# A causal attention block with sixteen routed experts on one core: turns, products and copies in other places of the issue order

## Chip, cores and metric

One of the cores of a Trainium2 chip runs the whole program in one launch. The metric is the device time of that core in microseconds (us). The kernel before takes 1741.03 us, the median of three runs (1738.7 to 1745.79). All arithmetic is in 32-bit floats.

## What is computed

```python
# x: 4 sequences of 1024 tokens, 256 wide; 16 heads of 64
proj = x @ W_in.T + b_in                      # q, k, v of all heads
q, k = rope(q, sin, cos), rope(k, sin, cos)   # y_lo = lo*cos + hi*sin; y_hi = hi*cos - lo*sin
att = softmax(mask(q @ k.T / 8))              # causal
x = layernorm(x + (att @ v) @ W_out.T + b_out)
gates = top 3 of softmax(x @ gate), scaled to sum to 1      # of 16 experts
x = layernorm(x + sum over the 3 of gate * (relu(x @ W1 + b1) @ W2 + b2))
```

## The kernel before, in words

**Two halves.** `attention` (from line 89) works through 32 pairs of heads, n = 0 to 31, eight pairs to a sequence. `moe` (from line 830) then works through 56 tiles of 256 tokens, each with one expert's weights. In both, the order of the instructions on TensorE (PE) is the order in which they are written. The other engines' order comes from a scheduler that takes what is ready first, within the ties that the program adds. Each engine then runs its own list in order, and waits on semaphores where an operand or a buffer isn't free.

**A pair has six slots**, k = 0 to 5 (loop at line 432). The 1024 queries of the pair are cut into eight chunks of 128; `chunks` (line 411) gives slot 0 chunk 7, slot 1 chunk 6, slot 2 chunk 5, slot 3 chunk 4, slot 4 chunks 3 and 2, and slot 5 chunks 1 and 0. In a slot:

- `scores` (line 279) multiplies q and k on PE into PSUM tiles of 512 columns (tag "s"). For each tile VectorE (DVE) scales, masks and takes the row minimum of the negated scores (line 308, tile `nmax`), writing P to SBUF. ScalarE (ACT) takes the exponential (line 323). `divide` (line 334) has DVE invert the row sums (line 337) and GpSimd (POOL) multiply P by them (line 340).
- `turn` (line 349) has DVE transpose P in blocks of 32, two slots after its scores, into `t_first` (keys 0 to 511) or `t_last` (keys 512 to 1023). `rows` holds the turns of a slot, and `turns` takes off the first entry, for both heads.
- `product(n, j)` (line 364) is P times V on PE for key chunk j. Slots 3, 4, 5 take j = 7, 6, 5 of pair n; slots 0, 1, 2 of the next pair take 4 and 3, 2, 1 and 0. It reads V from `vr`.
- `out` (line 397) is the output projection of two row blocks, summed into `acc` by DVE (line 468, called the sum here).
- `project(n+1, i, g)` (line 198) makes half g of the next pair's q (i = 0) or k (i = 1): four matmuls into a PSUM tile `pp` (also tag "s"); DVE's bias-and-sin product (line 220); ACT's plain copy with bias, `rawq` or `rawk` (line 226); and, once the tile is whole, four DMAs that write it back with its 32-row blocks swapped, `swq` or `swk` (line 234). k is projected in slots 0 and 1, so `swk` is issued in slot 1; q in slots 2 and 5. `rotate` (line 236) multiplies the swapped copy by cos and adds it, on DVE for k of pair 0 and on POOL otherwise.
- `values` (line 247) projects V, and DMAs write it to DRAM (`v_d`). `spread(n, g)` (line 271) loads half g back with four DMAs of 256 KB, one to each block of 32 partitions: `vr`. The four for g = 1, issued in slot 1, serve products 7 to 4; the four for g = 0, issued in slot 4, serve 3 to 0. There is one buffer for each g.

**PSUM.** All tiles of tag "s" share four buffers, in turn: scores, `pp`, `oo` of the output projection and `vv` of the values. In slot 0 they are four score tiles, `oo`, `pp`; slot 1's four score tiles so take the buffers of slot 0's third and fourth score tile, its `oo` and its `pp`.

**The SyncE (SP) queue** issues nearly all DMAs, in order; one that has to wait holds those behind it. `late(...)` (line 118) ties a DMA behind whatever was written last for the same queue, so the scheduler can't pull it forward. Loads of `wo` (line 143), `vr` (line 275), the third use of `wqk` and later (line 135) and `wv` are tied so; the `swk` and `swq` copies are not tied themselves.

**Orders by hand.** `after(i, kind)` (line 330) puts an instruction behind the last one of that kind in the issue order, with no wait. `divide` comes last in a slot, and `project` of k is tied behind the inverse.

**One-time steps.** `residual` (line 175) adds the output bias to half of `acc` on POOL. `plan` holds the router's steps; `first[2]` turns the first list of token numbers on PE (line 798). `moe.run` (line 949) gathers and loads six tiles, calls `last_norm` (the layernorm of the last sequence, lines 70 to 86) through `begun`, and then turns the first tile of tokens on PE and DVE (lines 884 and 886).

Of the kernel before, what the change touches and what calls it, by code (L numbers as in the profile page):

```python
# [88 lines left out]
def attention(  # L89
# [4 lines left out]
    nc = tc.nc  # L94
    with ExitStack() as ctx:
# [17 lines left out]
        ps_s = pool("ps_s", 4, space=PSUM)  # L113
# [84 lines left out]
        def project(n, i, g, kind=None):  # L198


            b, p = divmod(n, NP)
            if i == 0:
                half = rot[n, 0, g] = qkp.tile([P, 512], FP, tag=f"rotq{g}", name="rotq")
                part = raw = qkp.tile([P, 512], FP, tag="rawq", name="rawq")
                whole = True
            else:
                whole = (n, 1) in rot
                if not whole:
                    rot[n, 1] = qkp.tile([P, T], FP, tag="rotk", name="rotk")
                    raws[n] = qkp.tile([P, T], FP, tag="rawk", name="rawk", bufs=1)  # L210
                half, raw = rot[n, 1][:, ts(g, 512)], raws[n]
                part = raw[:, ts(g, 512)]
            ps = ps_s.tile([P, 512], FP, tag="s", name="pp")
            for c in range(DC):
                nc.tensor.matmul(  # L215
                    ps, lhsT=wqk[n][:, c, i, :], rhs=xts[b, g][:, c, :],
                    start=(c == 0), stop=(c == DC - 1),
                )
            bias = bqk[:, i, p : p + 1]
            m = nc.vector.scalar_tensor_tensor(  # L220
                half, ps, bias, sin[:, ts(g, 512)], ALU.add, ALU.mult
            )
            if kind:
                after(m, kind)
                order["part"] = m
            nc.scalar.activation(part, ps, AF.Identity, bias=bias)
            if whole:

                if i == 0:
                    swp = swps[n, 0, g] = qkp.tile([P, 512], FP, tag="swq", name="swq")  # L230
                else:
                    swp = swps[n, 1] = qkp.tile([P, T], FP, tag="swk", name="swk", bufs=1)
                for r in range(4):
                    nc.sync.dma_start(out=swp[ts(r, 32), :], in_=raw[ts(r ^ 1, 32), :])

        def rotate(n, i, g=None):
            key = (n, i) if i else (n, i, g)
            swp, res = swps.pop(key), rot[key]
            eng = nc.vector if n == 0 and i else nc.gpsimd
            first = eng.tensor_tensor(  # L240
                swp, swp, cos if i else cos[:, ts(g, 512)], ALU.mult
            )
            if "divide" in order:
                after(first, "divide")
            eng.tensor_tensor(res, res, swp, ALU.add)  # L245
# [175 lines left out]
        plan = {}  # L421
# [5 lines left out]
        with tc.manual_schedule(engines={mybir.EngineType.PE}):  # L427
            for n in range(n_pairs + 2):
                b, p = divmod(n, NP)
                if n == 2:  # L430
                    load_router()
                for k in range(n_slots):
                    here, before, ahead = (one_of(n + i) for i in (0, -1, 1))
                    part, ends, last = None, [], "scores"
                    if k == 2 and before:
                        product(n - 1, 1)
                    if here:
                        ends = scores(n, chunks[k])

                    m, kk = divmod(n * n_slots + k - 2, n_slots)  # L440
                    rows = [(qc, h) for h in (1, 0) for qc in chunks[kk] if qc >= 4 * h]

                    def turns(last):
                        qc, h = rows.pop(0)
                        for hh in range(2 if one_of(m) else 0):
                            turn(m, qc, hh, h, last)
                            last = "turn"
                        return last

                    if k == 2:  # L450
                        last = turns(last)

                    if k in (2, 5) and ahead:
                        project(n + 1, 0, int(k == 2), last)
                        last = "part"
                    if k < 3 and before:
                        product(n - 1, (4, 2, 0)[k])
                        if k == 2:
                            close(n - 1)
                    if k >= 3 and here:  # L460
                        product(n, 10 - k)
                    if k in (0, 3, 4, 5) and one_of(n - 1 - (k == 0)):
                        part = out(n - 1 - (k == 0), (k - 3) % 4 if k else 3)
                    if k != 2:
                        last = turns(last)
                    if part:
                        a, ps = part
                        order["sum"] = after(nc.vector.tensor_tensor(a, ps, a, ALU.add), last)
                        last = "sum"
                    while rows:  # L470
                        last = turns(last)
                    divide(n, ends, last)

                    if k == 0 and one_of(n + 2) and n % 2 == 0:
                        late(load_v(n + 2))
                    if k == 1 and one_of(n):
                        late(load_o(n))
                        spread(n, 1)
                        if one_of(n + 2):
                            late(load_qk(n + 2))  # L480
                    if k == 4 and one_of(n):
                        spread(n, 0)

                    if ahead:
                        if k < 2:
                            project(n + 1, 1, k, "inverse")
                        elif k == 2:
                            rotate(n + 1, 1)
                        elif k == 3:
                            rotate(n + 1, 0, 1)  # L490
                    if k == 0 and one_of(n):
                        rotate(n, 0, 0)
                    if k == 0 and before:
                        product(n - 1, 3)
                    m = n + 2 - n % 2
                    if k in (3, 4) and one_of(m):
                        values(m, 2 * (n % 2) + k - 3)
                    if k in (1, 2) and n == 0:
                        values(0, k - 1)
                    if k in (0, 4):  # L500
                        if n < 2 and k == 4 * (1 - n):
                            residual(0, n)
                        if p == NP - 1 and b + 1 < B:
                            residual(b + 1, k // 4)
                    for go in plan.pop((n, k), []):
                        go()
                    if k == 1 and p == 1 and 0 < b < B:
                        normalise(b - 1, sp)
                        steps, place, scatters = router.batch(
                            b - 1, accs[b - 1], ps_s, "s", ps_s, "s"  # L510
                        )
                        for i, go in enumerate(steps):
                            plan[n + i // 2, (3, 5, 1, 3)[i]] = [go]
                        plan[n + 2, 3] = [place]
                        for i in range(3):
                            for slot, c0, c1 in ((0, 0, 2), (1, 2, 4), (5, 4, 8)):
                                plan[n + 3 + i, slot] = scatters[8 * i + c0 : 8 * i + c1]
                        if b == B - 1:
                            plan[n + 6, 1] = [lambda: first.extend(router.first_list())]
                            plan[n + 6, 3] = [  # L520
                                lambda: first[1](router.on_dve), lambda: first[2](ps_s, "s")
                            ]
                if b + 1 < B:
                    if p == 3:
                        load_acc(b + 1)
                    if p == 4:
                        late(load_x(b + 1, 0))
                    if p == 6:
                        late(load_x(b + 1, 1))
            assert not plan  # L530
# [299 lines left out]
def moe(tc, router, first, last_norm, acc, ident, eps_t, wall, x_a, x_b, sums, out):  # L830
    nc = tc.nc
    with ExitStack() as ctx:
# [116 lines left out]
        def run(t0, t1, begun=lambda: None):  # L949
            with tc.manual_schedule(engines={mybir.EngineType.PE}):  # L950
                for t in range(t0, t0 + 6):
                    gather(t)
                    if t < t0 + 4:
                        load(t)
                begun()
                turn(t0)
                for t in range(t0, t1):
                    if t + 4 < t1:
                        load(t + 4)
# [171 lines left out]
```

## Time and profile before

| what | value |
|---|---|
| median of three runs | 1741.03 us (1738.7 to 1745.79) |
| time of the profiled execution | 1742.73 us |
| its span, first to last instruction | 1740.8 us |
| mean granted clock of TensorE | 0.969 |
| busy in the span: DVE, ACT, POOL | 1169.2, 716.2, 1106.4 us |
| HBM read and written | 183.17 and 52.79 MB |

The profile is one execution, times counted from the start of its span. A line of the timeline gives start, duration, engine, source line, operation, output tile <- input tiles, shape and count, and in brackets the idle time of the engine just before it with what ended it. PEld is the load of weights into TensorE, which runs beside the matmuls; SPq is SP's issue of DMAs, which is not the transfer itself. Matmuls are pipelined, and one that waits inside a group makes the group longer, without a bracket.

### The profile page before, as it was taken

Reading aid. Unit: us, or ns where it says so; the run is one execution under the profiler, and the core shown is the slowest. Engines: PE = TensorE matmul, PEld = TensorE weight load, DVE = VectorE, ACT = ScalarE, POOL = GpSimd, SP = SyncE. Lnnn points to the kernel's source line nnn. Section 1 sums busy time; section 2 is a strip of 40 time slices with the busy share of each in tenths; the row PEclk is TensorE's granted clock in tenths of the full one; section 3 lists DMA queues with packets and bytes.
Section 4 is the critical chain, followed back from the end, with each engine's and each line's share of the span. In section 5 each row is a group of like instructions: output and inputs, shape, how many; then the busy total and the mean of one; then the engine's idle time right before and its main releaser. Section 6 shows DMA issues by size and latency. Waiting matters only on the chain. (4 is left out here: it accounts for less than half of the span.)

```text
span 1740.8 us, 51881 instructions
## 1 busy us (share of the span) xinstructions
PE 1606.5 (92%) x20920; PEld 1097.8 (63%) x20920; DVE 1169.2 (67%) x3516; ACT 716.2 (41%) x1634; POOL 1106.4 (64%) x1050
## 2 busy tenths in 40 slices
PE   7899999989899998989999898999899999999970
PEld 3556556656556565655655565565588888888860
DVE  4678878888888788888887888888655222222224
ACT  3445445544444455445454554454322222222214
POOL 2656565754468865646786454588557778888544
PEclk9999999999999999999999999999899999999995
DMA  6454644464355546535554553444668998989857
GB/s 186 110 144 123 166 120 123 120 198 110 93 134 142 127 111 187 126 83 141 128 144 117 145 154 96 102 119 103 206 202 191 227 241 245 246 238 245 215 96 268
DMA packets 118166, 272.96 MB, mean 157 GB/s; under 512 B 21873, under 2 KB 72433, under 8 KB 102562
## 3 DMA queue, kind: packets, MB, share of 16 engines
q1 hardware_dynamic: 93122, 239.91, 49.8%
q0 software_dynamic: 24656, 29.68, 9.4%
q8 instruction: 167, 2.74, 0.7%
q14 instruction: 77, 0.63, 0.1%
q10 hardware_dynamic: 144, 0.01, 0.0%
HBM read 183.17 MB, written 52.79 MB: 136 GB/s over the span
## 5 line engine op out<-in xcount | busy, mean ns | idle before, releaser
L340 POOL TENSOR_SCALAR p<-p,rinv 128x512 f32<-128x512 f32 (+7 forms) x512 | 374.8, 747 | 436.0 <-DVE rinv L337 432.0
L323 ACT ACTIVATE p<-p,nmax 128x512 f32<-128x512 f32 (+7 forms) x512 | 391.9, 766 | 468.3 <-DVE nmax L308 446.9
L300 PE MATMUL s<-rotk,rotq 64*128 64x512 f32 (+3 forms) x1536 | 338.1, 522 | 21.9 <-POOL rotq L245 10.3
L357 DVE STREAM_TRANSPOSE t_first<-p 128x512 f32<-128x512 f32 (+3 forms) x512 | 276.7, 583 | 26.9 <-PE y_ps L378 26.3
L215 PE MATMUL pp<-xT,wqk 128*128 128x512 f32 x512 | 258.6, 630 | 35.8 <-DVE nmax L308 20.5
L300 PEld LDWEIGHTS s<-rotk,rotq 64*128 64x128 f32 x1536 | 152.7, 188 | 172.2 <-issue 96.9
L378 PEld LDWEIGHTS y_ps<-t_first,vr 32*64 32x64 f32 x8192 | 164.6, 133 | 101.3 <-DVE t_first L357 31.3
L378 PE MATMUL y_ps<-t_first,vr 32*64 32x160 f32 (+1 forms) x8192 | 222.0, 346 | 4.0 <-DVE t_first L357 3.8
L308 DVE CUSTOM_DVE_ANT_0 p<-s,zero 128x512 f32<-128x512 f32 x256 | 165.6, 683 | 87.6 <-PE s L300 87.6
L901 ACT ACTIVATE hid<-ps,w 128x256 f32<-128x256 f32 x224 | 93.9, 470 | 314.6 <-issue 252.2
L917 DVE TENSOR_TENSOR y<-ps,w 128x512 f32<-128x512 f32 x56 | 38.7, 691 | 274.5 <-PE ps L912 274.5
L926 POOL DMA_INDIRECT sums<-y,ids x112 | 178.4, 1592 | 69.1 <-DVE y L922 37.8
L896 PE MATMUL ps<-xg,w 128*128 128x256 f32 x896 | 204.4, 382 | 2.7 <-DVE xg L886 2.7
L912 PE MATMUL ps<-w,hid 128*128 128x256 f32 x896 | 202.6, 379 | 0.0
L912 PEld LDWEIGHTS ps<-w,hid 128*128 128x128 f32 x896 | 169.9, 190 | 22.9
L896 PEld LDWEIGHTS ps<-xg,w 128*128 128x128 f32 x896 | 167.1, 191 | 23.7 <-DVE xg L886 2.9
L215 PEld LDWEIGHTS pp<-xT,wqk 128*128 128x128 f32 x512 | 92.2, 195 | 130.7 <-issue 67.2
L378 PEld LDWEIGHTS y_ps<-t_last,vr 32*64 32x64 f32 x7424 | 113.7, 133 | 79.4 <-issue 64.4
L400 PE MATMUL oo<-wo,yT 128*128 128x256 f32 x512 | 147.1, 412 | 6.4 <-DVE nmax L308 4.6
L378 PE MATMUL y_ps<-t_last,vr 32*64 32x96 f32 (+3 forms) x7424 | 139.5, 253 | 3.3 <-ACT yT L391 0.6
L308 DVE CUSTOM_DVE_ANT_0 p<-s,mask,nmax 128x512 f32<-128x512 f32 (+3 forms) x256 | 130.3, 546 | 0.9 <-issue 0.5
L254 PE MATMUL vv<-wv,xT 128*128 128x256 f32 x512 | 121.3, 380 | 4.8 <-DVE nmax L308 4.8
(147 smaller groups left out, 1890.3 us busy)
## 6 DMA issues: line engine op xcount, KB each, us to landing
vr<-v_d SPq DMA_DIRECT2D x256, 256.0 KB
w<-in_wall_dram SPq DMA_DIRECT2D x56, 1154.0 KB
swk<-rawk SPq DMA_DIRECT2D x128, 128.0 KB
swq<-rawq SPq DMA_DIRECT2D x256, 64.0 KB
v_d<-v SPq DMA_DIRECT2D x128, 128.0 KB
wqk<-in_w_qk_dram SPq DMA_DIRECT2D x32, 256.0 KB
xT<-in_xT_dram SPq DMA_DIRECT2D x8, 512.0 KB
wv<-in_w_v_dram SPq DMA_DIRECT2D x16, 256.0 KB
```

Of the source, the lines that this page charges most:

```text
L215: nc.tensor.matmul(ps, lhsT=wqk[n][:, c, i, :], rhs=xts[b, g][:, c, :], start=(c == 0), stop=(c == DC - 1),)
L254: nc.tensor.matmul(ps[:, u, :], lhsT=xts[b, cc // 2][:, c, ts(cc % 2 * 2 + u, P)], rhs=wv[n][:, c, :], start=(c == 0), stop=(c == DC - 1),)
L300: nc.tensor.matmul(s[:, :n_k], lhsT=rot[n, 0, qc // 4][ts(hh, KD), ts(qc % 4, P)], rhs=k[ts(hh, KD), ds(k0, n_k)], start=True, stop=True,)
L308: i = nc.vector.tensor_tensor_reduce(out=probs[n, qc, hh][:, ds(k0, n_k)], in0=s[:, :n_k], in1=mask[:, 512 - n_k :] if last else zero[:, : ...
L323: nc.scalar.activation(pr, pr, AF.Exp, bias=m, scale=-1.0, accum_out=rsum[:, hh : hh + 1])
L340: order["divide"] = router.behind = nc.gpsimd.tensor_scalar(pr, pr, rinv[:, hh : hh + 1], 1.0, ALU.mult, ALU.mult)
L357: order["turn"] = router.on_dve = after(nc.vector.transpose(turned[n][h][:, hh, :, ds(i - 4 * h, n_j, step=7 - 4 * h), :], probs[n, i, hh] ...
L378: nc.tensor.matmul(st[n][a][ts(hh, KD), ds(32 * j, 32 * (TC - j))], lhsT=vrs[n, h][ts(a, 32), jh // 2 * 8 + 2 * u + jh % 2, ts(hh, KD)], r ...
L400: nc.tensor.matmul(ps[:, v, :], lhsT=st[n][:, ts(2 * h + v, P)], rhs=wo[n], start=True, stop=True,)
L896: nc.tensor.matmul(ps[:, f - f0, :], lhsT=w[:, ds(c * FF + f * P, P)], rhs=xg[:, c, :], start=(c == 0), stop=(c == DC - 1),)
L912: nc.tensor.matmul(ps[:, h, :], lhsT=hid[:, f, ts(h, P)], rhs=w[:, ds(W2_AT + f * D, D)], start=(f == 0), stop=(f == FC - 1),)
L926: s = behind(nc.gpsimd.indirect_dma_start(out=sums[t % 2], out_offset=bass.IndirectOffsetOnAxis(ap=ids[:, h, i : i + 1], axis=0), in_=y[:, ...
```

## The change

- In slot 5 the first turn goes ahead of the bias-and-sin product of q, as it already did in slot 2; the second turn then comes ahead of the sum.
- In slots 0 and 1 the projection of the next pair's k is written directly behind the sum (slot 0) or the first turn (slot 1), ahead of the remaining turns and of the inverse. It was written behind `divide` and behind the loads of `wo`, `vr` and `wqk`. All that `project` issues moves with it: the four matmuls, DVE's product, ACT's copy, and in slot 1 the four `swk` DMAs. PE's order stays as it was, as nothing else for PE lay between.
- The swap copies of q of pair 0 are issued from ACT's queue instead of SP's; k of pair 1 is rotated on DVE instead of POOL.
- The two bias sums of the first sequence move from pair 0 slot 4 and pair 1 slot 0 to pair 1 slot 5 and pair 2 slot 4.
- The turn of the first token list moves from slot 3 to slot 4 of pair 31.
- In `moe.run` the turn of the first tile goes ahead of `begun`, the last layernorm.

```diff
@@ project
+                eng = nc.scalar if n == 0 and i == 0 else nc.sync
                 for r in range(4):
-                    nc.sync.dma_start(out=swp[ts(r, 32), :], in_=raw[ts(r ^ 1, 32), :])
+                    eng.dma_start(out=swp[ts(r, 32), :], in_=raw[ts(r ^ 1, 32), :])
@@ rotate
-            eng = nc.vector if n == 0 and i else nc.gpsimd
+            eng = nc.vector if n < 2 and i else nc.gpsimd
@@ the loop over slots
-                    if k == 2:
+                    if k in (2, 5):
                         last = turns(last)
...
-                    if k != 2:
+                    if k != 2 and rows:
                         last = turns(last)
                     if part:
                         a, ps = part
                         order["sum"] = after(nc.vector.tensor_tensor(a, ps, a, ALU.add), last)
                         last = "sum"
+
+                    if k < 2 and ahead:
+                        project(n + 1, 1, k, last)
+                        last = "part"
                     while rows:
                         last = turns(last)
                     divide(n, ends, last)
...
                     if ahead:
-                        if k < 2:
-                            project(n + 1, 1, k, "inverse")
-                        elif k == 2:
+                        if k == 2:
                             rotate(n + 1, 1)
...
+                    if (n, k) in ((1, 5), (2, 4)):
+                        residual(0, n - 1)
                     if k in (0, 4):
-                        if n < 2 and k == 4 * (1 - n):
-                            residual(0, n)
...
-                            plan[n + 6, 3] = [
-                                lambda: first[1](router.on_dve), lambda: first[2](ps_s, "s")
-                            ]
+                            plan[n + 6, 3] = [lambda: first[1](router.on_dve)]
+                            plan[n + 6, 4] = [lambda: first[2](ps_s, "s")]
@@ moe.run
+                turn(t0)
                 begun()
-                turn(t0)
```

## The prediction

> **What bounds the kernel now.** I read the page first, then PE's timeline through the attention half, then the other engines and SP's queue over one pair, and the windows for what the DMA engines carry.
>
> ```profile
> PE 1606.5 (92%) x20920; PEld 1097.8 (63%) x20920; DVE 1169.2 (67%) x3516; ACT 716.2 (41%) x1634; POOL 1106.4 (64%) x1050
> ```
>
> PE is the longest by far, so an edit pays only where PE stands, or runs slow inside a group. The chain that ended last covers 2% of the span and only the last layernorm, so it doesn't help here. An undisturbed pair in PE's timeline, slots 1 to 4:
>
> ```profile
> 251.74 2.59 PE L300 MATMUL s<-rotk,rotq 64*128 64x512 f32 x8
> 254.26 1.56 PE L378 MATMUL y_ps<-t_first,vr 32*64 32x192 f32 x64
> 255.75 1.98 PE L215 MATMUL pp<-xT,wqk 128*128 128x512 f32 x4
> 257.66 1.77 PE L378 MATMUL y_ps<-t_first,vr 32*64 32x224 f32 x64
> 259.36 1.56 PE L300 MATMUL s<-rotk,rotq 64*128 64x512 f32 x8
> 261.27 1.99 PE L215 MATMUL pp<-xT,wqk 128*128 128x512 f32 x4 [0.35 <-DVE nmax L308]
> 263.19 1.98 PE L378 MATMUL y_ps<-t_first,vr 32*64 32x256 f32 x64
> 265.10 1.35 PE L300 MATMUL s<-rotk,rotq 64*128 64x512 f32 x8
> 266.38 1.15 PE L378 MATMUL y_ps<-t_last,vr 32*64 32x32 f32 x40
> ...
> 270.24 1.77 PE L300 MATMUL s<-rotk,rotq 64*128 64x512 f32 x8
> ```
>
> Groups follow one another with one bracket of 0.35 in 35.85 us. But the first score group (slot 1) takes 2.59 where the last (slot 4, also 512 and 384 columns for both heads) takes 1.77: 0.8 us are lost inside. PE's weight loads name the cause:
>
> ```profile
> 253.42 0.29 PEld L300 LDWEIGHTS s<-rotk,rotq 64*128 64x128 f32 x2 [0.53 <-ACT rawk L226]
> ```
>
> The fourth score tile takes the PSUM buffer of slot 0's `pp`, which ACT's copy frees only at 253.37. That copy follows DVE's product at 251.91, which stands behind the sum (250.35), two turns (1.02) and the inverse. So DVE's order in slot 0 costs PE 0.8 us. PE's timeline lists 19 such whole slot 1 groups (2.46 to 2.60); with those split by a query's edge I count 21 of 32 pairs.
>
> Now SP's queue:
>
> ```profile
> 96.15 2.47 SPq L234 DMA_DIRECT2D swq<-rawq  x4
> 98.67 0.58 SPq L549 DMA_DIRECT2D dump<-in_dump_dram  x1
> ...
> 248.76 0.36 SPq L143 DMA_DIRECT2D wo<-in_w_outT_dram  x1
> 249.16 1.86 SPq L275 DMA_DIRECT2D vr<-v_d  x4
> 251.07 0.42 SPq L135 DMA_DIRECT2D wqk<-in_w_qk_dram  x1
> 259.30 2.41 SPq L234 DMA_DIRECT2D swk<-rawk  x4
> ```
>
> The `vr` of products 7 to 4 is asked for at 249.16, as soon as product 4 of the pair before has freed the buffer, and product 7 (40 matmuls at 266.38) needs all four parts: 17.2 us of room. SP then stands until ACT's second `rawk` (258.55, 0.69 long). The first two lines show that a tied load keeps its place: `dump` waits for nothing, and yet goes out right behind the swaps written before it. The windows show what the transfer takes:
>
> ```profile
> 250.00:256.00 6.00, 6.00 (x139) 3.56 (x138) 5.75 (x17) 2.86 (x6) 3.83 (x4) 1.00 1.02 233
> 256.00:257.00 1.00, 1.00 (x3) 0.42 (x3) 0.35 (x2) 1.00 (x2) 0.90 (x1) 1.00 0.09 29
> 257.00:260.00 3.00, 3.00 (x70) 1.73 (x70) 0.92 (x2) 0.71 (x2) 2.00 (x2) 1.00 0.00 0
> ```
>
> The last two columns are the DMA engines' share and GB/s: full for 6.0 us, 233 GB/s x 6 = 1.40 MB, which is `wo` + 4 `vr` + `wqk` (0.125 + 1.05 + 0.26), then nothing. By proportion `vr` has landed by 250 + 6 x 1.18/1.44 = 254.9, at the latest at 256.1: 5.8 to 6.9 us behind its first issue. I take 6.4.
>
> **The change, part by part.**
>
> *k's product behind the sum, slot 0.* DVE can start it when the sum (about 250.95) and `pp` (about 250.4) are done, so 1.0 sooner; ACT's copy ends near 252.4 and not 253.37. The fourth tile's first load would want it about 252.9. The two turns and the inverse move 0.7 later; DVE stood 0.25 before slot 1's first reduction and ACT's exponential had ended, so nothing becomes late, and POOL, which stood 3.77 before that division, has room. Gain 0.8 a pair, and about 0.05 from product 3, which just waited for a turn: 0.85 x 21 = **-18**. If DVE had no room, the 0.7 would return as later reductions and the gain would be near zero.
>
> *The turn sooner, slot 5.* DVE stood 0.72 for `pp` and 0.87 for `oo` there; turns of 0.49 and 1.29 fill both. The sum still starts about when `oo` is done (280.4 against 280.49), and DVE is free for slot 0 about 1 us sooner. This is cover for the step above and is already in it: 0. Without that cover (pairs with router work on DVE) the sum is 1.3 late, and so is a buffer of slot 0: up to +1.3 in six pairs, down to 0; I take 0.
>
> *k's project in slot 1: its four DMAs.* Here more moves than DVE's product. `swk` is now written ahead of `wo`, `vr` and `wqk`, and these are tied behind what SP was given last. SP so waits for `rawk` first, and the three loads stand behind it, whose buffers have been free for 10 us. Counted in this pair's times: `rawk` ends 259.24, `swk` is issued 259.30 to 261.71, `wo` takes 0.36, the first `vr` goes out about 262.1 and the fourth lands 6.4 later at 268.5. PE wants it at 266.38: **a wait of 2.1 us** that isn't there today. DVE can't shorten it: its product already follows `pp` at once in slot 1 (0.55 of idle for PE), and both ends move together if slot 1's scores get faster. In the other pairs the end of the `swk` issues lies 2.0 to 5.4 ahead of product 7 (middle 4.66, mean 4.2), so the wait is 0.4 + 6.4 less that: mean 2.6. Some issues are slow where other transfers were in flight, so I take 2.3; bounds 1.4 (landing in 5.8, usual distance) and 3.3 (landings of 7 to 8 us). Pairs 0 to 30 have it: 31 x 2.3 = **+71**. Nothing later gives it back: output, values and slot 4's scores follow on PE, and DVE and POOL only get slack.
>
> [...]
>
> *Pair 0 to 1.* PE stands longest here:
>
> ```profile
> 60.02 3.79 PE L300 MATMUL s<-rotk,rotq 64*128 64x512 f32 x8 [6.28 <-POOL rotq L245]
> ```
>
> POOL had k's rotation (2.37 + 2.35) and a bias sum (2.34) ahead of that rotation of q; both leave, 7.1 in all, so the 6.3 go. DVE gets 1.22 + 1.23 (its rows for pair 0's rotation) in slots 2 to 3, where it stood only 0.33; up to +2.1 if PE followed at once, down to 0 because product 7 waits for `vr` then: I take 0. The bias sum in pair 2 slot 4 can hold that pair's next sum: divisions end near 280 in the pattern above, plus 2.35 is 282.3 against a sum at 280.4: +1.5. Together **-5**. The q swaps on ACT start at about 14.9 and not 15.78, but hold ACT's next copies 0.6 each: -0.9 to +1, taken as 0.
>
> *One-time turns.* `ids` (PE idle 2.35 at 1236.47): its data is there by slot 4, **-2**. The last norm: PE stood 2.65 before 1269.67 for a DVE copy behind 2.70 + 0.62 of statistics: **-2**, between -2.6 and 0. Pair 2's slot 1, where `rawk` was late by 1.45: **-1**.
>
> Sum: 71 - 18 - 5 - 2 - 2 - 1 = +43. The profiled execution is 1742.7 (span 1740.8 and 1.9 around), so 1786; the median of the runs is 1.7 below it, so **1784**.
>
> **Rivals.**
>
> *The loads are in time (faster).* Either the scheduler issues `vr` at its old place, or the four parts land within 4.3 us (266.4 - 262.1). Then only the gains are left: 1741 - 28 = 1713. [...] Against it: the tied loads keep their place wherever I looked[...]. The point of decision is 4.3 us from first issue to landing.
>
> *Wait and gain cancel.* A landing in about 5.1 us gives 0.8 to 0.9 of wait a pair (31 x 0.9 = 28) against 28 of gains: 1741. Nothing in the row is that fast.
>
> *The wait is larger and gains are lost.* If landings take 7.4 (other transfers in the same stretch) the wait is 3.3: 102 - 28 = +74, 1815. Against: the DMA engines were idle from 257 to 260 and only `swk` is ahead.
>
> **Chances.** Forecast case 0.80 (about 1760 to 1806: waits of 1.6 to 3.0), in time 0.10, cancelled 0.05, larger 0.05. The range 1750 to 1810 leaves out the first rival and the top. Faster by over 0.5% (8.7 us, about what a measurement of this kernel can tell from no change) 0.10, within 0.05, slower 0.85.
>
> **What would show it.** Right: in SP's timeline `swk`, then `wo`, `vr`, `wqk`; PE idle about 2 us before `y_ps` with `t_last` 32x32 in every pair, put down to the DMA of `vr`; slot 1's scores at 1.7 to 1.8; no 6.28 at pair 1; ACT's `rawk` behind DVE's product as before. A pair of 37.2 to 37.5 us for 35.85. Wrong: `vr` still issued in slot 0, or that product starting with no idle time; or slot 1's scores still at 2.6, which would mean that another buffer held them.

## The result, and the profile after

The changed kernel takes **1904.18 us** (median of four runs, 1897.27 to 1913.42) where the kernel before, run beside it, takes 1742.99 (1738.7 to 1745.79): a ratio of 1.0944, interval 1.0917 to 1.0971, so 161 us slower. 43 were forecast. The profiled execution took 1909.57 us; its span is 1907.8 us, the mean granted clock of TensorE (the share of its full speed at which it was let run) 0.922, for 0.969 before. Executions over 1.5% longer than the shortest of the same kernel are left out of the times and ratios below (on the chip of 1821.92 us eleven of the kernel before, with a granted clock of 0.946 to 0.951, where the others had 0.951 to 0.959).

From the page of the kernel before, the groups to compare (busy time and mean ns of one, then the idle time just before them with what ended most of it):

```profile
L378 PE MATMUL y_ps<-t_last,vr 32*64 32x96 f32 (+3 forms) x7424 | 139.5, 253 | 3.3 <-ACT yT L391 0.6
L400 PE MATMUL oo<-wo,yT 128*128 128x256 f32 x512 | 147.1, 412 | 6.4 <-DVE nmax L308 4.6
L254 PE MATMUL vv<-wv,xT 128*128 128x256 f32 x512 | 121.3, 380 | 4.8 <-DVE nmax L308 4.8
```

The page of the kernel after, busy time of the engines and the same groups, two lines further down in the program:

```profile
PE 1671.2 (88%) x20920; PEld 1150.9 (60%) x20920; DVE 1176.5 (62%) x3518; ACT 716.1 (38%) x1634; POOL 1103.5 (58%) x1048
...
L380 PE MATMUL y_ps<-t_last,vr 32*64 32x96 f32 (+3 forms) x7424 | 169.7, 263 | 122.9 <-DMA vr<-v_d 109.9
...
L402 PE MATMUL oo<-wo,yT 128*128 128x256 f32 x512 | 174.0, 471 | 4.0 <-DVE nmax L310 2.3
L256 PE MATMUL vv<-wv,xT 128*128 128x256 f32 x512 | 154.7, 457 | 0.9 <-DVE nmax L310 0.6
```

There are two things to see. PE stood 109.9 us for `vr`, a wait that the kernel before did not have. And PE, with the same 20920 matmuls, was *busy* 64.7 us longer (1671.2 against 1606.5): one matmul of the output projection took 471 ns (412 before), one of the values 457 ns (380). The span is 167 us longer: 64.7 of busy time and 102.3 of idle time.

SP's queue of the kernel after, slot 1 of one undisturbed pair:

```profile
281.14 2.41 SPq L236 DMA_DIRECT2D swk<-rawk  x4
283.65 0.53 SPq L143 DMA_DIRECT2D wo<-in_w_outT_dram  x1
284.22 3.37 SPq L277 DMA_DIRECT2D vr<-v_d  x4
```

`swk` stands ahead of `wo` and `vr`, as the prediction read from the order of the text. PE's timeline over the same stretch:

```profile
286.93 1.35 PE L302 MATMUL s<-rotk,rotq 64*128 64x512 f32 x8
289.25 0.27 PE L380 MATMUL y_ps<-t_last,vr 32*64 32x32 f32 x2 [0.97 <-DVE nmax L310]
290.36 0.27 PE L380 MATMUL y_ps<-t_last,vr 32*64 32x32 f32 x2 [0.84 <-DMA vr<-v_d]
291.58 0.39 PE L380 MATMUL y_ps<-t_last,vr 32*64 32x32 f32 x2 [0.95 <-DMA vr<-v_d]
292.72 1.08 PE L380 MATMUL y_ps<-t_last,vr 32*64 32x32 f32 x34 [0.75 <-DMA vr<-v_d]
293.73 2.07 PE L402 MATMUL oo<-wo,yT 128*128 128x256 f32 x4
295.60 2.96 PE L256 MATMUL vv<-wv,xT 128*128 128x256 f32 x8
298.49 1.77 PE L302 MATMUL s<-rotk,rotq 64*128 64x512 f32 x8
```

The four parts of `vr` land one after another, 1.1 to 1.2 us apart. PE does two matmuls with each of the first three and stands in between. The first bracket names DVE, but `nmax` frees nothing that this product needs: the trace has the landings (the last count of each part's semaphore) at 289.11, 290.22, 291.44 and 292.58, and each of the four groups starts 0.14 us behind one of them. The last part is there for PE at 292.72, 8.5 us behind the first issue at 284.22. After the wait, the same four matmuls of `oo` take 2.07 us (1.13 undisturbed) and the eight of `vv` 2.96 (1.89). The windows of the kernel after show the clock (columns: window, its length, then busy time of PE, PEld, DVE, ACT, POOL with counts, then granted clock, DMA share, GB/s):

```profile
289.00:290.00 1.00, 0.27 (x2) 0.19 (x2) 1.00 (x7) 0.00 (x0) 1.00 (x2) 1.00 1.07 238
290.00:291.00 1.00, 0.27 (x2) 0.19 (x2) 1.00 (x6) 0.89 (x3) 1.00 (x2) 0.97 1.09 221
291.00:292.00 1.00, 0.39 (x2) 0.29 (x2) 0.24 (x1) 0.85 (x3) 1.00 (x1) 0.50 0.76 156
...
296.00:297.00 1.00, 1.00 (x4) 0.79 (x3) 1.00 (x2) 0.00 (x0) 0.00 (x0) 0.50 0.00 0
297.00:298.00 1.00, 1.00 (x5) 0.80 (x4) 0.80 (x3) 0.00 (x0) 0.11 (x1) 0.62 0.00 0
298.00:299.00 1.00, 1.00 (x5) 0.46 (x5) 0.00 (x0) 0.40 (x1) 1.00 (x2) 1.00 0.00 0
```

The granted clock falls to 0.50 at about 290.9 and is back at 297.8: 6.8 us at half speed, 3.4 of them lost, and that for waits of 3.5 us in all. Over the span, the clock's record has 299.3 us at half clock after and 108.8 before: (299.3 - 108.8) / 2 = 95 us of lost PE clock, part of which lies over time in which PE stood anyway.

Theory then: the order on SP's queue costs the 161 us and all the gains besides, one part as PE's wait for `vr`, the other as half clock behind it. Rivals: the longer waits come from DVE's or ACT's new order (then moving the loads cures nothing), or the half clock has nothing to do with the wait.

### The profile page after: what moved, and what is told of

Read it like the earlier page. It is cut to its first block, busy times and chain, and to the rows that moved or that the text cites. A ratio compares the mean times of both kernels' runs of the same rounds, so it can differ in the third digit from the quotient of the medians.

```text
span 1907.8 us, 51877 instructions
## 1 busy us (share of the span) xinstructions
PE 1671.2 (88%) x20920; PEld 1150.9 (60%) x20920; DVE 1176.5 (62%) x3518; ACT 716.1 (38%) x1634; POOL 1103.5 (58%) x1048
## 5 line engine op out<-in xcount | busy, mean ns | idle before, releaser
L302 PE MATMUL s<-rotk,rotq 64*128 64x512 f32 (+3 forms) x1536 | 319.2, 518 | 14.5 <-ACT rawq L226 4.6
L380 PE MATMUL y_ps<-t_last,vr 32*64 32x96 f32 (+3 forms) x7424 | 169.7, 263 | 122.9 <-DMA vr<-v_d 109.9
L380 PEld LDWEIGHTS y_ps<-t_last,vr 32*64 32x64 f32 x7424 | 138.0, 144 | 203.2 <-issue 141.3
L302 PEld LDWEIGHTS s<-rotk,rotq 64*128 64x128 f32 x1536 | 145.3, 189 | 156.7 <-issue 96.3
L380 PEld LDWEIGHTS y_ps<-t_first,vr 32*64 32x64 f32 x8192 | 159.9, 131 | 98.9 <-issue 63.5
L380 PE MATMUL y_ps<-t_first,vr 32*64 32x160 f32 (+1 forms) x8192 | 216.0, 342 | 2.8 <-DVE t_first L359 2.3
L470 DVE TENSOR_TENSOR acc<-oo,acc 128x512 f32<-128x512 f32 x128 | 86.1, 672 | 164.1 <-PE oo L402 161.8
L402 PE MATMUL oo<-wo,yT 128*128 128x256 f32 x512 | 174.0, 471 | 4.0 <-DVE nmax L310 2.3
L256 PE MATMUL vv<-wv,xT 128*128 128x256 f32 x512 | 154.7, 457 | 0.9 <-DVE nmax L310 0.6
```

Source lines behind the costliest of these rows:

```text
L256: nc.tensor.matmul(ps[:, u, :], lhsT=xts[b, cc // 2][:, c, ts(cc % 2 * 2 + u, P)], rhs=wv[n][:, c, :], start=(c == 0), stop=(c == DC - 1),)
L302: nc.tensor.matmul(s[:, :n_k], lhsT=rot[n, 0, qc // 4][ts(hh, KD), ts(qc % 4, P)], rhs=k[ts(hh, KD), ds(k0, n_k)], start=True, stop=True,)
L380: nc.tensor.matmul(st[n][a][ts(hh, KD), ds(32 * j, 32 * (TC - j))], lhsT=vrs[n, h][ts(a, 32), jh // 2 * 8 + 2 * u + jh % 2, ts(hh, KD)], r ...
L402: nc.tensor.matmul(ps[:, v, :], lhsT=st[n][:, ts(2 * h + v, P)], rhs=wo[n], start=True, stop=True,)
```

## The experiments

Four of them (the loads ahead again, the order alone, half of the copies, the wait filled) ran together on a chip where the kernel before itself takes 1821.92 us, with executions from 1803.36 to 1835.49, so ratios count there; the run with both parts of DVE's order had 1800.08 beside it, all others about 1740. The expectations name times beside 1743. A period is from the first matmul of product 4 (slot 0) to that of the next pair, unless product 7 (slot 3) is named; the undisturbed pairs counted singly are pairs 2 to 7.

**The loads ahead again.** The changed kernel with the tied loads back ahead of k's project; nothing else differs.

```diff
+                    if k == 1 and one_of(n):
+                        late(load_o(n))
+                        spread(n, 1)
+                        if one_of(n + 2):
+                            late(load_qk(n + 2))
                     if k < 2 and ahead:
                         project(n + 1, 1, k, last)
...
-                    if k == 1 and one_of(n):
-                        late(load_o(n))
-                        ...
```

> The changed kernel with only this taken back: in slot 1 the loads of wo, vr and wqk are again written ahead of the projection of k, so ahead of its four swk copies on SP's queue. Queue theory (the loss is vr behind swk: 3.5 us of idle PE before product 7 in a pair, and 2.9 us more because the matmuls behind it run at half clock): all of the loss goes and only the gains stay, about 1713 (1700 to 1725). Rival, DVE order (k's product ahead of turns and inverse makes P late): stays at 1890 to 1904, as DVE's order is untouched. A mix of both would lie between.

Measured 1812.21 us, a ratio of 0.9951 (0.992 to 0.9982). All of the loss is gone, but of the gains less than a third came (0.983 was expected). The wait for `vr` is gone from the list of waits. What is left at this line is another wait, put down to `issue`, which is time in which PE waited for nothing that the profile shows; it stands before products 4 to 1 and not before product 7:

```profile
PE y_ps L380 <- issue: 20.5, 44, 1.6
```

**The same kernel and the changed one, together on a chip like the first.**

> The changed kernel with the loads of wo, vr and wqk ahead of the projection, once more, for its time beside the two halves of the change on one chip. The gains of both halves add: 0.983 (0.977 to 0.988). [...]

> The changed kernel as it is, beside the others on one chip: 1.094 (1.08 to 1.11). The difference to the version with the loads first is then the whole price of the queue's order: about 0.11 of the time before, 190 us.

With the loads ahead 1726.76 us, 0.9932 (0.9914 to 0.995), so again less gain than the 0.983 expected; the changed kernel 1913.21, 1.0998 (1.0973 to 1.1023). One change of place on one queue so is 1913.21 - 1726.76 = **186 us**. From the two profiles, span 1917.4 against 1727.6: 189.8 us, of which PE's busy time has 76.7 (1675.5 against 1598.8) and its idle time 113.1, where the wait for `vr` alone is 115.7. The half clock is 310.9 us against 114.4. A pair with the loads ahead, PE's timeline:

```profile
254.31 1.35 PE L302 MATMUL s<-rotk,rotq 64*128 64x512 f32 x8
255.59 1.15 PE L380 MATMUL y_ps<-t_last,vr 32*64 32x32 f32 x40
256.67 1.13 PE L402 MATMUL oo<-wo,yT 128*128 128x256 f32 x4
257.64 1.89 PE L256 MATMUL vv<-wv,xT 128*128 128x256 f32 x8
259.46 1.77 PE L302 MATMUL s<-rotk,rotq 64*128 64x512 f32 x8
```

and its SP queue:

```profile
238.86 0.36 SPq L143 DMA_DIRECT2D wo<-in_w_outT_dram  x1
239.26 2.46 SPq L277 DMA_DIRECT2D vr<-v_d  x4
241.76 0.42 SPq L135 DMA_DIRECT2D wqk<-in_w_qk_dram  x1
248.52 2.42 SPq L236 DMA_DIRECT2D swk<-rawk  x4
```

`vr` goes out 16.3 us ahead of product 7, in the changed kernel 4.1 (284.22 to the end of the scores, 288.28). The period is 35.0 us, in pairs 3 to 8 of the changed kernel 40.5 to 41.4.

**The order alone, in the kernel before.** This puts only the tied loads behind k's project in slot 1.

```diff
-                    if k == 1 and one_of(n):
-                        late(load_o(n))
-                        ...
...
                         if k < 2:
                             project(n + 1, 1, k, "inverse")
+                            if k == 1 and one_of(n):
+                                late(load_o(n))
+                                ...
```

> The kernel before with one edit: in slot 1 the loads of wo, vr and wqk are written behind the projection of k; DVE's order and all else as before. Queue theory: all of the loss without the gains, 1743 + 161 + about 28 = 1930 (1905 to 1945), vr going out behind swk and PE idle before product 7. DVE-order rival: 1743, nothing changes.

Measured 2017.67 us, 1.1124 (1.1022 to 1.1225), for 1930/1743 = 1.107 expected: 196 us over 1821.92, and its shortest execution (2015.05) is 180 us over the longest of the kernel before on this chip. DVE, ACT and POOL have the order of the kernel before here, so the rival that blames their new order falls. The list of waits:

```profile
PE y_ps L378 <- DMA vr<-v_d: 105.5, 95, 7.2
```

**Half of the copies ahead.** The changed kernel with two `swk` copies ahead of the loads and two behind, so that `vr` goes out about 1.2 us sooner.

```diff
-                for r in range(4):
-                    eng.dma_start(out=swp[ts(r, 32), :], in_=raw[ts(r ^ 1, 32), :])
+                def copies(rs):
+                    for r in rs:
+                        eng.dma_start(out=swp[ts(r, 32), :], in_=raw[ts(r ^ 1, 32), :])
+                if i and n > 0:
+                    copies((0, 1))
+                    return lambda: copies((2, 3))
+                copies(range(4))
@@ the loop over slots, behind the loads
+                    if rest:
+                        rest()
...
```

> The changed kernel, but from pair 1 on only two of k's four swk copies go ahead of the loads of wo, vr and wqk, two behind them. vr goes out 1.2 us sooner, so the idle time before product 7 falls from about 3.5 to 2.3 us a pair: 31 x 1.2 = 37 us. If the half clock comes only when a longer stretch is nearly empty, most of the 2.9 us a pair behind the wait goes too: 1790 to 1830. If matmuls slow down in proportion to the idle time, a third of it goes: 1840 to 1850. DVE-order rival: 1900.

Measured 1939.49 us, 1.0673 (1.0571 to 1.0776). The two answers were 1.027 to 1.050 and 1.056 to 1.061; the measured ratio lies over both, nearer to the second. Its pairs 2 to 7, sorted by period (here from product 7 to product 7), show the wait for `vr` (the brackets of PE's timeline) and the half clock (the clock's record) apart:

| period, us | waits for `vr` | at half clock | period less wait, less half of the half clock |
|---|---|---|---|
| 36.83 | 1.73 | 0 | 35.1 |
| 37.97 | 1.23 | 3.41 | 35.0 |
| 38.69 | 1.39 | 0 | 37.3 (1.07 of it a wait for `acc`) |
| 38.88 | 2.21 | 3.41 | 35.0 |
| 40.68 | 2.33 | 6.83 | 34.9 |
| 40.73 | 2.90 | 6.83 | 34.4 |

The half clock came in pieces of 3.41 us here, none, one or two, each for 1.7 us of time. The size of the wait alone doesn't say how many: 1.23 had one piece, 1.73 none. In the table all waits of 2.2 us and more have some, but pair 24 of the changed kernel waited 2.27 us (0.36, 1.13 and 0.78) and had none, where its pair 2 had 6.83 us of half clock behind 2.19.

**The wait filled.** The changed kernel, with slot 3's output and values ahead of product 7 on PE, so that PE has about 2.8 us of work while `vr` lands.

```diff
-                    if k >= 3 and here:
+                    if k >= 4 and here:
                         product(n, 10 - k)
...
                         values(m, 2 * (n % 2) + k - 3)
+                    if k == 3 and here:
+                        product(n, 7)
```

> The changed kernel with PE's order in slot 3 changed: the output projection (about 1.0 us) and the values (1.9 us) come ahead of product 7 instead of behind it, so PE works while vr lands; the queue's order is as changed. Queue theory: the idle time falls from 3.5 to about 0.6 us in a pair and the half clock goes, as PE is never empty for long: 1713 + 31 x 0.6 = 1732 (1715 to 1760). If the half clock stayed in spite of a short wait, about 1820. DVE-order rival: 1900.

Measured 1845.96 us, 1.017 (0.9955 to 1.0386), from two executions only (1833.09 and 1858.84). The interval contains 1, so it is unclear whether it is slower than the kernel before; the ratio lies over the 0.984 to 1.010 expected. It is far below the run with half of the copies beside it (1939.49). Its trace (of an execution of 1862.04 us), one pair:

```profile
186.66 1.10 PE L402 MATMUL oo<-wo,yT 128*128 128x256 f32 x4 [0.96 <-ACT yT L393]
187.60 1.89 PE L256 MATMUL vv<-wv,xT 128*128 128x256 f32 x8
189.42 0.31 PE L380 MATMUL y_ps<-t_last,vr 32*64 32x32 f32 x6
189.98 0.68 PE L380 MATMUL y_ps<-t_last,vr 32*64 32x32 f32 x34 [0.25 <-DMA vr<-v_d]
```

The load comes as late as in the changed kernel, yet `oo` takes 1.10 and `vv` 1.89, and pairs 2 to 7 take 35.5 to 36.8 us from product 7 to product 7 with no half clock. The filled wait left a new one (0.96 for ACT's `yT`). In pair 9, with the steps of a layernorm, 3.65 us of wait for `vr` stay, half clock stays too (the eight matmuls of `x_ps` behind it take 1.97 us, in the next pair 1.04), and the period is 53.1 us for 44.8 in the kernel before. So the half clock does follow the wait, and the rival that it has another cause falls for the undisturbed pairs.

**The gains: DVE's order alone.** The kernel before with the slot 5 turn and both products of k ahead, the loads kept ahead of k's project.

```diff
-                    if k == 2:
+                    if k in (2, 5):
                         last = turns(last)
...
+                    if k == 1 and one_of(n):
+                        late(load_o(n))
+                        ...
+                    if k < 2 and ahead:
+                        project(n + 1, 1, k, last)
+                        last = "part"
...
```

> The kernel before with only DVE's order changed: the turn sooner in slot 5 and k's product behind the sum, with the loads of wo, vr and wqk kept ahead of the projection. None of the swaps, rotations, bias sums, list turn or first-tile turn is moved. If the order costs DVE nothing and frees slot 0's pp in time, 35.0 us in an undisturbed pair for 35.85, about 18 to 22 us in all: 0.988 of the time before (0.985 to 0.991). If the order by itself costs (turns and inverse late): 1.000 or more.

Measured 1738.96 us, 0.9995 (0.9983 to 1.0007): the forecast 0.988 is missed, the gain isn't there. By what was expected, the order then costs as much as it gains; two of the next runs ask where.

**The gains: the one-time parts alone.** The kernel before with the swaps on ACT, k of pair 1 on DVE, the later bias sums, the later list turn and the earlier turn of the first tile.

```diff
+                eng = nc.scalar if n == 0 and i == 0 else nc.sync
...
-            eng = nc.vector if n == 0 and i else nc.gpsimd
+            eng = nc.vector if n < 2 and i else nc.gpsimd
...
+                    if (n, k) in ((1, 5), (2, 4)):
+                        residual(0, n - 1)
...
+                turn(t0)
                 begun()
-                turn(t0)
...
```

> The kernel before with only the one-time parts of the change: q's swaps of pair 0 on ACT, k of pair 1 rotated on DVE, the two bias sums later, the list turned one slot later, the first tile turned ahead of the last norm. Pairs keep their 35.85 us. Gain by the prediction's sum 5 + 2 + 2 + 1 = 10 us: 0.994 (0.992 to 0.998). If the idle time that they remove also brought the half clock behind it, some 3 us more each at pair 1, the list and the tile: 0.990.

Measured 1729.2 us, 0.9944 (0.9923 to 0.9965), 10.1 us: as forecast.

**DVE's order taken apart.** Two kernels from the one before, one with the slot 5 turn alone, one with slot 0's product alone:

```diff
@@ the turn alone
-                    if k == 2:
+                    if k in (2, 5):
                         last = turns(last)
...
-                    if k != 2:
+                    if k != 2 and rows:
                         last = turns(last)
@@ slot 0's product alone
+                    if k == 0 and ahead:
+                        project(n + 1, 1, 0, last)
+                        last = "part"
...
-                        if k < 2:
+                        if k == 1:
                             project(n + 1, 1, k, "inverse")
```

> The kernel before with only the slot 5 turn ahead of q's product. Theory: this turn fills idle time of DVE in undisturbed pairs, so they stay at 35.85 us; if it is this part that makes the pairs with router and layernorm work later (layernorm pairs 43.0 for 42.2 us), the ratio is above 1, about 1.003. If slot 0 does that, the ratio is 1.000.

> The kernel before with only slot 0's product of k behind the sum; slot 1 and slot 5 as before, so no load changes its place. Theory: the fourth score tile of slot 1 gets its buffer sooner, undisturbed pairs 35.0 us for 35.85. If the slot 5 turn gave the gain back, the ratio here is 0.990; if DVE's order in slot 0 itself costs the other pairs as much as it gains (as in the run with both), it is 0.999.

The turn: 1739.2 us beside 1740.68, 0.999 (0.998 to 1.0). Slot 0's product: 1729.69 us, 0.9935 (0.9921 to 0.9948). Most undisturbed pairs take 35.0 to 35.2 us in *both*: each alone frees slot 1's fourth score tile in time, and the 0.85 can be had once only. They part in the six pairs with router steps on DVE (10, 11, 18, 19, 26, 27; each from its product 7 to the next): summed over those, the turn is 6.7 us longer than before and the product 4.2 shorter. In the three such periods with a layernorm (from pairs 8, 16, 24) it is the other way: the turn 0.5 shorter, the product 3.6 longer. PE's timeline in the first router pair, slot 5, in the kernel before:

```profile
438.72 1.44 PE L300 MATMUL s<-rotk,rotq 64*128 64x512 f32 x4 [1.03 <-DVE nmax L308]
440.74 2.66 PE L300 MATMUL s<-rotk,rotq 64*128 64x512 f32 x4 [0.59 <-ACT rawq L226]
443.33 2.01 PE L378 MATMUL y_ps<-t_last,vr 32*64 32x128 f32 x64
```

with the turn:

```profile
433.60 1.44 PE L300 MATMUL s<-rotk,rotq 64*128 64x512 f32 x4 [1.04 <-DVE nmax L308]
436.15 3.23 PE L300 MATMUL s<-rotk,rotq 64*128 64x512 f32 x4 [1.12 <-ACT rawq L226]
439.31 2.01 PE L378 MATMUL y_ps<-t_last,vr 32*64 32x128 f32 x64
```

and with slot 0's product:

```profile
432.85 1.43 PE L300 MATMUL s<-rotk,rotq 64*128 64x512 f32 x4 [1.04 <-DVE nmax L308]
434.88 1.70 PE L300 MATMUL s<-rotk,rotq 64*128 64x512 f32 x4 [0.59 <-ACT rawq L226]
436.51 1.21 PE L378 MATMUL y_ps<-t_last,vr 32*64 32x128 f32 x64
```

In slot 5 the turn stands ahead of q's product, ACT's `rawq` follows that product, and PE's second half of the scores needs the buffer that `rawq` frees: the wait is 0.53 us longer than in both others. The half clock behind it (3.23 and 2.01 for 1.70 and 1.21) isn't the turn's alone, as the kernel before has it too (2.66 and 2.01) behind the same 0.59 that left none with the product. What comes back in every kernel with the turn is the idle time: over the six pairs PE stood 31.8 us with the turn alone, 31.7 and 31.9 in the two kernels that have k's product as well, 27.3 in the kernel before and 26.3 with slot 0's product alone. In the pair shown, the turn moved forward on DVE moved the next step back, as the 0.53 us for `rawq` show.

**Both parts of DVE's order, slot 1 as before.** The two edits above in one kernel.

> The kernel before with the slot 5 turn and slot 0's product of k, slot 1 as before. Each alone made undisturbed pairs 35.0 us, by the same 0.85, so they should not add; alone the turn cost the pairs with router steps 6.7 us in all and slot 0's product gained 4.2 there. If the turn gives back the gain of slot 0's product, the ratio is 0.999; if slot 1's product did that in the run with all three (0.9995), it is 0.993.

Measured 1796.13 us beside 1800.08 on its chip, 0.9978 (0.9958 to 0.9999). It lies between the two answers, nearer to the one that blames the turn, and on another chip; it does not settle how the rest divides between the turn and slot 1's product.

**The best parts together.** The one-time parts and slot 0's product, nothing else.

> The one-time parts together with slot 0's product of k behind the sum, nothing else: the gains without the moved loads, the slot 1 product and the slot 5 turn. If the gains add, 0.9944 x 0.990 = 0.985; if slot 0's gain is given back, 0.994.

Measured **1716.07 us** beside 1740.68, 0.9866 (0.9851 to 0.9881): 1.3% faster than the kernel before, and faster than the changed one. The two gains add: 0.9944 x 0.9935 = 0.9879, inside the interval.

## Why the prediction was right or wrong

It had the direction, the queue, the wait and its place; the size was short by 118 us (161 against 43), nearly all of it in one term: 71 us were put down for what cost 186.

- **"`swk` is now written ahead of `wo`, `vr` and `wqk`": right.** SP's queue shows it. Putting the loads back removes all of the loss, and putting them behind in the kernel before brings 196 us.
- **"The fourth lands 6.4 later": short.** In pairs 2 to 7 of the kernel after, from `vr`'s first issue to the start of the last group of product 7 took 7.0, 7.2, 8.2, 7.1, 8.5 and 7.0 us. The traces of before and after agree on this: in the kernel before, the semaphore of the fourth part is full at 256.42 in the pair that the prediction read, 7.3 us behind the first issue and later than its latest bound, though the window from 256 to 257 shows a DMA share of only 0.09; over pairs 0 to 30 these landings took 6.9 us and more there, in the median 8.2, and 8.05 in the kernel after. So the copies ahead made `vr` late by its issue and not by a slower transfer. Idle time at product 7 of pairs 2 to 7 is 2.1 to 3.5 us, mean 2.7, for 2.3.
- **"Pairs 0 to 30 have it: 31 x 2.3 = +71": the step that failed.** The number of pairs was right and the wait in a quiet pair nearly so, but the term put nothing for what the wait does to the matmuls behind it. "Nothing later gives it back: output, values and slot 4's scores follow on PE" is true, and yet these run at half clock for 6.83 us: 3.4 us more a pair. Between the profiles with and without the moved loads, PE's busy time differs by 76.7 us, for which the term had nothing. The idle part itself was 110 and not 71: before and within product 7 PE stands 8.4 to 9.0 us in pairs 9, 17 and 25, which have a layernorm, and 4.0 to 5.3 us in pairs 12 to 14, 20 to 22, 28 and 29, and the forecast had one mean for all, with the short landing in it. A quiet pair then sums well: 35.0, and 2.4 of wait, and 3.4 of clock make 40.8, and the trace has 40.6.
- **The half clock could be seen before.** The line of the pair 0 to 1 that the prediction shows has eight score matmuls in 3.79 us, where the same eight take 1.99 in an undisturbed pair. It stood behind a wait of 6.28, and the prediction read the bracket and not the duration. Likewise 367.97 of the kernel before, a `pp` group of 2.75 us for 1.98 behind 3.49 of idle time. The mean clock of 0.969, in the table, was 108.8 us at half clock, of which 47.3 lie behind PE's last matmul.
- **Half clock behind short gaps.** In the pair shown no gap is longer than 1.0 us (0.97, 0.84, 0.95 and 0.75), with two matmuls between each and the next, and yet 6.83 us of half clock follow: waits broken by two matmuls at a time have it too. At 3.4 us a pair that makes 31 x 3.4 = 105; the clock's record has 95 more than before over the whole span. What decides whether a wait has it isn't shown: waits of 1.2 to 1.7 us, and of 2.2 to 2.3, came with half clock and without, and no run sets the cause apart.
- **"Gain 0.8 a pair ... -18": right for a quiet pair, wrong in the sum.** The period goes from 35.85 to 35.0, but with all three parts of DVE's order nothing is left in the whole (0.9995). Slot 0's product alone gives 11.0 us (1740.68 less 1729.69).
- **"This is cover for the step above and is already in it: 0" (the slot 5 turn): wrong.** It is no cover but another way to the same 0.85, and in the six pairs with router work it costs 6.7 us alone, 1.1 a pair. The prediction's own bound, +1.3, has that size, but partly by luck: it was reckoned from a late sum, and the added wait shown is for `rawq`.
- **One-time parts, -5 - 2 - 2 - 1 = -10: right in the sum** (10.1 measured). The parts were not run singly. By the traces of the kernel before and of this one, which may be from two chips, the stretch of pairs 0 and 1 (product 7 to product 7) is 6.3 us shorter, for 6 forecast, and all behind product 7 of pair 31 is 8.9 shorter, for 4 forecast (kernels without these parts differ there by 1.0 to 3.5 too), with some 3 us lost in other pairs: that the sum fits so well is partly luck.
- **Rivals.** In time, or cancelling: wrong, by the landing. The wait of 3.3 a pair (1815) had nearly the right idle time, 3.5 a pair over the span, and nothing for the half clock either.

Open: in the traces with the slot 5 turn, PE has waits put down to `issue` in single pairs (4.7 us in 5 places with the turn alone), where its list in the kernel before has none. They may be from other chips, and slot 0's product alone has 1.0 us in 2 places, so it isn't shown that the turn is the cause. This line is from the kernel with DVE's order alone:

```profile
872.78 1.05 PE L378 MATMUL y_ps<-t_first,vr 32*64 32x224 f32 x16 [2.69 <-issue]
```

The period of that pair is 40.6 us, with the turn alone 37.9, with slot 0's product alone 36.2. No run shows what PE waited for there.

## What to carry to other kernels

When a step moves in the text, list its DMAs first: the compute that moved here was worth 0.85 us a pair, and four copies ahead of a tied load cost 186 us in all. Take a transfer's time up to the landing of its last part; the DMA engines' share had fallen before that (0.09 from 256 to 257 in the kernel before, where the last part landed at 256.42). Price a new wait on TensorE with its after-effect (here 3.4 us of clock behind 2.4 of wait in a quiet pair): look in the profile for groups behind the waits that exist already, compare their duration with the same shape undisturbed, and add that to the new waits, as a bound, since not every wait had it. Two edits that free the same buffer were one gain here (35.0 to 35.2 us in most undisturbed pairs with either alone), and each is to be priced apart in the pairs with other work on its engine (the six router pairs: 6.7 us longer in sum with the turn, 4.2 shorter with slot 0's product).

## What was not expected of the hardware

- Behind the waits of pairs 2 to 7 of the kernel after, half clock came in stretches of 6.83 us, twice 3.41; over its whole span the clock's record has 3.41, 6.83, 10.24 and 13.65 us (9, 27, 1 and 2 times) and one last stretch behind PE's last matmul. In those six pairs it followed gaps of 0.3 to 2.0 us that had two matmuls of 0.13 us between them, 2.1 to 3.5 us of idle time together. In the pair shown with the wait filled, with 0.96 and 0.25 us of idle time apart, there was none.
- In pairs 2 to 7 of the kernel after, PE started with the last of four loads of 256 KB 7.0 to 8.5 us behind the first issue. In the pair shown, the DMA engines' share was 1.07 and 1.09 in two of the windows, at 238 and 221 GB/s; other transfers ran beside the loads (from 284 to 294 the windows add up to 1.88 MB, of which `vr` is 1.05).
- The kernel before takes 1740, 1800 or 1822 us on different chips. On the last, with the loads ahead, PE stood 20.5 us in 44 places, put down to `issue`, before the later products; on the first sort of chip the same kernel had 4.8 us of it in 4.
